# A graph layer whose gathers count on semaphores set up by hand

## The chip, the cores and the metric

The kernel runs on one core of a Trainium2 chip. The time is that of one execution on the device in microseconds; the kernel before took 4658.97 us (median of 3 runs, 4657.78 to 4659.96). Five engines of the core appear below: TensorE (PE in the profile), VectorE (DVE), ScalarE (ACT), GpSimd (POOL) and SyncE (SP). Each works through its own instructions in the order in which they stand, and they wait for each other on semaphores.

## The reference

A message-passing layer with 12,500 nodes and 400,000 edges, which come sorted by their target node. In short:

```python
h = concat(s @ lin1_ws * a / 8, (v @ lin1_wv) * a / sqrt(32))      # 160 numbers per node
hid = silu(edge_scalars @ fc_w1 / 8)                               # 64 per edge
w1, w2, w3, w4, w5 = split(hid @ fc_w2 / 8)                        # 64+64+32+32+32 per edge
es, ev = h_s[src], h_v[src]                                        # the gather
m_s1 = w1 * es * e0;  m_s2 = w4 * dot(ev, e1) / 3
m_v1 = (w2 * es) x e1;  m_v2 = w3 * ev * e0;  m_v3 = w5 * cross(ev, e1) / 2
agg = segment_sum([m_s1, m_s2, m_v1, m_v2, m_v3], dst) / 4
o = agg @ lin2 * a;  pre = (self-connection of x) + o
out = layernorm(x + concat(silu(pre_s[:64]), sigmoid(pre_s[64:96]) * pre_v))
```

`e0` and `e1` are the one and the three components of the 4 edge attributes, `a` a number per node.

## The kernel before

The 400,000 edges are cut into 3125 tiles of 128 edges, one edge per partition. Four tiles make a quad, so the main loop, unrolled in Python, has 782 steps, and 24 tiles make a chunk. Indices and edge attributes are loaded for 48 tiles at a time (`AHEAD`). The order of each engine's instructions is the order in which the program is written; the framework adds the semaphore waits. Dependencies of engines on each other go through semaphores, one per engine; a DMA counts on one of eight lanes (DMASW0 to 7 for those that POOL issues, DMAHW0 to 7 for SP's), and a DMA that uses a lane waits for the one that used it before. Where an instruction needs more waits than it can carry itself, queue instructions (`EVENT_SEMAPHORE`, on the engine's queue: DVEq, POOLq) stand ahead of it and hold the rest.

First the node features are multiplied by `lin1` and written as the table `h_tab` to memory. Then, for each quad:

- POOL issues four gathers (line 476), one per tile, each of 128 rows of 160 numbers, from `h_tab` into a quarter of the buffer `hg`. The pool `deep` has six such buffers. A quad's first gather waits for VectorE, which must have read the buffer's former content; its third gather waits, from the seventh quad on, for the weights of the quad three before it (`weighed_by[n - 3]`, the "pace").
- TensorE computes the weights of the four tiles into PSUM, `pw` (line 551, two banks), from `hid`, the hidden layer that it computes every second quad (line 467) and ACT activates (line 469).
- VectorE compares (line 614) each edge's target, relative to its block of 16 nodes, with 0 to 15, which gives the one-hot matrix; it goes into the same bank as the weights. Then it multiplies weights and gathered rows (`pr`): one instruction of 128x512 for the scalars (line 561) and three of 128x384 for the vectors (line 569). Line 623 multiplies one-hot matrix and edge attributes into `sel`. Line 672 adds up results of earlier blocks.
- Two quads later TensorE multiplies `sel` by `pr` (line 630, `pa`), which is the sum over edges. ACT copies it out (line 863, `sa`), TensorE turns it (line 649), ACT copies that (line 652, `tt`), and TensorE applies the second layer (line 664).

The edge attributes come in the order of memory; `by_slot` (line 597) has ACT put them into the order of the steps, `eas`, once per 48 tiles, by six copies of 128x32, three quads before they are needed. SP reloads the indices (line 160), `eat` and the edge scalars.

Of the kernel before, what the change touches and what calls it, by code (L numbers as in the profile page):

```python
# [21 lines left out]
P = 128  # L22
# [9 lines left out]
W = 16  # L32
Q = 4
KB = 4
SIDE = KB * BT
CT = 2 * SIDE
# [25 lines left out]
def gnn_kernel(  # L62
# [21 lines left out]
    nc = tc.nc  # L84
# [21 lines left out]
    rel = consts.tile([P, TT], I16, name="rel")  # L106
# [60 lines left out]
    def index(t):  # L167
        a0, idx, _ = ahead(t)
        return idx[:, t - a0:t - a0 + 1]
# [67 lines left out]
    with tc.tile_pool(name="nodes", bufs=len(starts)) as nodes, tc.tile_pool(  # L237
        name="nodes_ps", bufs=6, space=PSUM
# [33 lines left out]
        for q in range(4):  # L272
            t0, s = divmod(q * QN, P)
            nc.gpsimd.dma_start(at_k[:P - s, q], attr[s:, t0:t0 + NQ])
            if s:
                m = min(NQ, NT - t0 - 1)
# [67 lines left out]
        for c0, cn, xw, xz in loaded:  # L344
# [7 lines left out]
            n = min(cn, P)  # L352
# [56 lines left out]
    for to, part, pieces, w, r0, c0, by in maps:  # L409
        for k, piece in enumerate(pieces):  # L410
# [3 lines left out]
            m = terms.setdefault((to, part, four), len(terms))  # L414
# [54 lines left out]
                nc.scalar.activation(hid[:k, c], ph[:k, c], AF.Silu, scale=1.0 / math.sqrt(64))  # L469
        return hid  # L470

    def gather(pool, idx, behind=None):

        hg = pool.tile([P, Q, D], F32, name="hg")
        for t, i in enumerate(idx):
            got = nc.gpsimd.indirect_dma_start(  # L476
                out=hg[:, t, :], out_offset=None, in_=h_tab,
                in_offset=bass.IndirectOffsetOnAxis(ap=i, axis=0))
            if behind and behind.get(t) is not None:
                tc.add_manual_dep(got.ins, behind[t], mybir.DependencyInfo(  # L480
                    mybir.DependencyClass.Sync, mybir.DependencyReason.DATA), reason="pace")
        return hg

    own = [n for n in range(OWN + EARLY + 6, len(steps) - 4, OWN) if len(steps[n][2]) == Q]
    by_bytes = h_tab.rearrange("n d -> (n d)").bitcast(U8)
# [102 lines left out]
    def by_slot(t):  # L588

        a0, _, eat = ahead(t)  # L590
        if a0 not in sorted_eat:
            n = min(AHEAD, TT - a0)
            eas = loads.tile([P, AHEAD, 4], F32, name="eas")
            m = n // CT
            for u in range(0, SIDE if m else 0, 2):
                o, i = eas[:, 2 * u:2 * u + 1], eat[:, u:u + 1]
                nc.scalar.copy(
                    bass.AP(tensor=o.tensor, offset=o.offset,
                            ap=[o.ap[0], [4 * CT, m], [4, 2], [8, 2], [1, 4]]),
                    bass.AP(tensor=i.tensor, offset=i.offset,  # L600
                            ap=[i.ap[0], [4 * CT, m], [4, 2], [4 * SIDE, 2], [1, 4]]))
            m *= CT
            for k in range(m, n):
                o = slot_of[a0 + k] - a0
                nc.scalar.copy(eas[:, o], eat[:, k])
            sorted_eat[a0] = eas
        return sorted_eat[a0]

    def one_hot(tiles, pw):

        n = len(tiles)
        t0 = slot_of[tiles[0][0]]
        oh = pw[:, :n, NWT:NWT + W]
        nc.vector.tensor_tensor(oh, rel[:, t0:t0 + n, None].to_broadcast([P, n, W]),  # L614
                                iota[:, None, :].to_broadcast([P, n, W]), op=OP.is_equal)
        return oh

    def select_quad(pool, tiles, oh):

# [160 lines left out]
    with tc.tile_pool(  # L780
        name="fin", bufs=1
    ) as fin, tc.tile_pool(
        name="mine", bufs=2
    ) as mine, tc.tile_pool(
        name="late", bufs=2
    ) as late, tc.tile_pool(name="edge", bufs=2) as edge, tc.tile_pool(
        name="deep", bufs=6
    ) as deep, tc.tile_pool(name="banks", bufs=1, space=PSUM) as banks:
        pw_ps = Banks(banks, "pw", Q * 256, 2)
        pa_ps = Banks(banks, "pa", 512, 2)  # L790
# [196 lines left out]
        with in_order:  # L987
            fetch(0)
            hide(0)
            hide(2)  # L990
            waits = []
            weighed_by, summed_by = {}, {}
            checks = farthest(late)
            for n, (c, i, tiles) in enumerate(steps):
                if 2 <= n < 2 + ZP // 2:
                    for k in range(2):
                        clear(2 * (n - 2) + k)
                if 1 <= n < 10:
                    scale(3)
                if n == 13:  # L1000
                    last_own = own_scalars_vectors(fin, *last_nodes)
                if n == 17:
                    connect_last(misc_ps, *last_nodes, *last_own)
                if n in checks:
                    checks[n]()
                if n == 0:
                    fetch(n + 6)
                fetch(n + LEAD)
                fetch_rows(n)
                hg = hq_of.pop(n) if n in own else gather(  # L1010
                    deep, [index(t) for t, _, _ in tiles], {2: weighed_by[n - 3] if n >= 7 else None})
                pw = weights(pw_ps, hids[c, i // 2], [(half, u - i // 2 * 4) for _, half, u in tiles])
                weighed_by[n] = weighed[-1]

                if n + 4 < len(steps) and not steps[n + 4][1] % 2:
                    hids_due.append((n, n + 4))
                if n + 3 < len(steps):
                    by_slot(steps[n + 3][2][0][0])
                rest = spread_out(n, 0)
                if gates_due and (gates_due[0][0] <= n or n + LATE >= len(steps)):  # L1020
                    assert not rest or n + LATE >= len(steps)
                    rest = [rest, gates_due.pop(0)[1]]
                elif rest:
                    rest = [rest]
                step_on = doing.pop(0) if doing and not turning and not rest and not gates_due else None
                ready = []

                def first(n=n):
                    for gate in reversed(rest or []):
                        if gate:  # L1030
                            gate()
                    ready.extend(add_up(n))

                if n + 3 >= len(steps):
                    while ready or adds and adds[0][0] <= n:
                        ready.extend(add_up(n))
                        add(*ready.pop(0))
                oh = one_hot(tiles, pw)
                sel = select_quad(edge, tiles, oh) if n + 2 >= len(steps) else None
                if n in own:  # L1040
                    hg = hg()
                pr = products(edge, pw, hg, len(tiles), [first, lambda n=n: ready.extend(add_up(n))])
                if not sel:
                    sel = select_quad(edge, tiles, oh)
                for a in ready:
                    add(*a)
                if step_on:
                    step_on()
                begin(n)
                some_rows(SLOTS[1])  # L1050
                waits.append((tiles, pr, sel))
                if n + 1 == len(steps):
                    for blocks, tt in due(maps_due, n):
                        output(n, blocks, tt)
                    for js, whole in due(turns_due, n):
                        turn_blocks(n, js, whole)
                while len(waits) > (2 if n + 4 < len(steps) else 1):
                    sum_up(n, *waits.pop(0))
                if n >= 2:
                    summed_by[n - 2] = summed[-1]  # L1060
                some_rows(SLOTS[2])
                spread_out(n, 1)
                some_rows(SLOTS[3])
            assert not scales and not hids_due and not gates_due
            assert not supply and not any(begun.values())
            nc.gpsimd.drain()
            last_steps = finish(fin, misc_ps, *last_job, most=LAST, pool=deep)
            n = len(steps)
            while waits:
                sum_up(n, *waits.pop(0))  # L1070
            while turns_due or maps_due:
                n += 1
                for blocks, tt in due(maps_due, n):
                    output(n, blocks, tt)
                for js, whole in due(turns_due, n):
                    turn_blocks(n, js, whole)
            assert len(adds) <= NO
# [20 lines left out]
        with tc.For_i(0, n_redo, 1):  # L1098
# [108 lines left out]
```

## Time and profile before

| what | value |
|---|---|
| time, median of 3 runs | 4658.97 us |
| time of the profiled execution | 4659.28 us |
| span of the profiled execution | 4657.5 us |
| TensorE busy, mean granted clock | 3852.9 us (83%), 0.870 |
| VectorE busy | 2369.7 us (51%) |
| ACT busy | 840.2 us (18%) |
| POOL busy | 2995.5 us (64%) |
| share of the DMA engines' time, gathers | 21.8% |
| share of the DMA engines' time, SP's transfers | 12.5% |

The span is the time from the first to the last instruction of the profiled execution; 1.8 us of its time lie outside. A row of a group reads: line, engine, operation, what it writes and reads, count, then busy us in total and ns of one, then the idle time of the engine ahead of such instructions and what ended most of it. "issue" means that nothing which the profile shows was waited for, "remote" that what released the wait can't be named. Matmuls' ends are modelled, and consecutive rows of one engine overlap a little. A row of a timeline reads: start, duration, engine, line, operation, and in brackets the idle time ahead of it and its releaser.

### The profile page before, as it was taken

The numbers are of one execution on the slowest core, as the hardware profiler recorded it, in microseconds if no ns is written. First come the engines' busy times: TensorE is split into PE (matmuls) and PEld (weight loads), VectorE is DVE, ScalarE is ACT, GpSimd is POOL, SyncE is SP. The second block draws the span as 40 slices with busy tenths as digits, with TensorE's granted clock in tenths as the row PEclk, the third lists the DMA queues.
The fourth block names the chain that finished last, engine by engine and source line by source line (L and its number), as shares of the span: only waits on it lengthen the run. The fifth ranks groups of instructions, "written<-read, shape, count | busy, mean of one in ns | idle before, by whom it ended". The sixth has DMA issues, their size and how long they took to land.

```text
span 4657.5 us, 53879 instructions
## 1 busy us (share of the span) xinstructions
PE 3852.9 (83%) x17955; PEld 1891.7 (41%) x17955; DVE 2369.7 (51%) x6412; ACT 840.2 (18%) x1872; POOL 2995.5 (64%) x3172
## 2 busy tenths in 40 slices
PE   5788888888888888888888888887888888888886
PEld 4343444444444334344443444343443444444443
DVE  5544554545545455454554555554554554554454
ACT  1211121211111111111111111111111111111112
POOL 6666666666666666666666666666666666666663
PEclk8888898888888898888888888888888898988888
DMA  6333333333333333333333333333333333333331
GB/s 208 93 79 79 95 86 81 94 78 88 95 78 89 87 84 88 90 84 86 90 85 85 89 88 85 89 87 79 93 88 79 93 80 87 95 78 88 86 87 48
DMA packets 237510, 412.26 MB, mean 89 GB/s; under 512 B 78040, under 2 KB 160961, under 8 KB 237093
## 3 DMA queue, kind: packets, MB, share of 16 engines
q0 software_dynamic: 152960, 266.64, 21.8%
q1 hardware_dynamic: 83668, 141.96, 12.5%
q8 instruction: 143, 2.34, 0.2%
q14 instruction: 145, 1.19, 0.1%
q10 hardware_dynamic: 594, 0.13, 0.0%
HBM read 392.49 MB, written 16.00 MB: 88 GB/s over the span
## 4 chain that ended last, share of the span: by engine, by line
PE 63%; issue 12%; another core or an unknown queue 10%; DVE 9%; DMA 2%; POOL 2%; ACT 1%; DVEq 0%; SPq 0%; ACTq 0%; POOLq 0%
PE pa L630 23%; PE pw L551 17%; PE misc L664 8%; PE misc L467 7%; PE misc L649 6%; DVE pr L569 5%; POOL hg L476 2%; PE misc L721 2%; DMA hg<-h_tab,idx 1%; DVE sel L623 1%; PE misc L717 1%; DVE pr L561 1%; DVE pw L614 1%; DMA xz<-in_xv_t_dram 1%
## 5 line engine op out<-in xcount | busy, mean ns | idle before, releaser
L476 POOL DMA_INDIRECT hg<-h_tab,idx x3125 | 2964.8, 949 | 1601.1 <-issue 824.7
L630 PE MATMUL pa<-pr,sel 128*64 128x416 f32 x6250 | 1546.6, 585 | 122.8 <-issue 118.5
L551 PE MATMUL pw<-w,hid 64*128 64x224 f32 x6250 | 1050.7, 408 | 382.9 <-issue 257.7
L614 DVE TENSOR_TENSOR pw<-rel,iota 128x64 f32<-128x64 int16 x782 | 180.1, 230 | 2143.1 <-remote 1114.7
L569 DVE TENSOR_TENSOR pr<-pw,hg 128x384 f32<-128x384 f32 x2346 | 1153.2, 547 | 0.0
L551 PEld LDWEIGHTS pw<-w,hid 64*128 64x128 f32 x6250 | 644.2, 203 | 1078.8 <-issue 742.1
L630 PEld LDWEIGHTS pa<-pr,sel 128*64 128x64 f32 x6250 | 444.4, 149 | 971.3 <-issue 924.5
L561 DVE TENSOR_TENSOR pr<-pw,hg 128x512 f32<-128x512 f32 x782 | 540.2, 691 | 30.3 <-DVE pw L614 1.9
L467 PE MATMUL misc<-es,w 128*128 128x512 f32 (+1 forms) x784 | 491.3, 709 | 30.5 <-DVE rel L429 19.6
L664 PE MATMUL misc<-tt,l 128*96 128x256 f32 (+5 forms) x1496 | 400.3, 411 | 42.8 <-issue 40.6
L469 ACT ACTIVATE hid<-misc 128x512 f32<-128x512 f32 x392 | 234.4, 598 | 977.3 <-remote 277.7
L652 ACT COPY tt<-misc 128x512 f32<-128x512 f32 (+1 forms) x263 | 153.0, 582 | 1426.5 <-remote 826.8
L863 ACT COPY sa<-pa 128x416 f32<-128x416 f32 x521 | 263.9, 507 | 714.2 <-remote 279.9
L649 PE MATMUL misc<-ident,sa 128*128 128x128 f32 (+1 forms) x1558 | 311.3, 290 | 76.6 <-ACT sa L863 42.3
L623 DVE TENSOR_TENSOR sel<-pw,eas 128x256 f32<-128x256 f32 x782 | 323.2, 413 | 0.1
L664 PEld LDWEIGHTS misc<-tt,l 128*96 128x96 f32 (+1 forms) x1496 | 241.9, 176 | 194.9 <-issue 125.9
L649 PEld LDWEIGHTS misc<-ident,sa 128*128 128x128 f32 x1558 | 218.5, 173 | 162.2 <-issue 100.5
L672 DVE TENSOR_TENSOR acc<-acc,os 96x32 f32 x1042 | 194.1, 186 | 53.4 <-remote 16.3
L467 PEld LDWEIGHTS misc<-es,w 128*128 128x128 f32 x784 | 129.3, 205 | 157.3 <-issue 131.7
L649 PE MATMUL misc<-first_last,sa 128*128 128x128 f32 x784 | 188.8, 297 | 4.3 <-issue 4.2
L717 PE MATMUL misc<-ident,acc 96*128 96x96 f32 x196 | 64.0, 332 | 95.7 <-DVE pw L614 68.3
L667 ACT COPY os<-misc 96x512 f32<-96x512 f32 (+2 forms) x68 | 38.4, 564 | 449.9 <-PE misc L664 168.7
(97 smaller groups left out, 852.1 us busy)
## 6 DMA issues: line engine op xcount, KB each, us to landing
es<-in_es_t_dram SPq DMA_DIRECT2D x258, 384.0 KB
hg<-h_tab,idx POOLq DMA_INDIRECT x3125
h_tab<-ht POOLq DMA_DIRECT2D x24, 320.0 KB
xt<-in_x_dram SPq DMA_DIRECT2D x23, 320.0 KB
out_dram<-y SPq DMA_DIRECT2D x23, 320.0 KB
xv<-in_xv_t_dram SPq DMA_DIRECT2D x23, 192.0 KB
eat<-in_ea_dram SPq DMA_DIRECT2D x41, 96.0 KB
xw<-in_xs_t_dram SPq DMA_DIRECT2D x6, 512.0 KB
```

The lines of the kernel that those rows point to most:

```text
L467: nc.tensor.matmul(ph[:k, c], w1[:k, :k], es[:k, t0 * P + c0 * P:t0 * P + c1 * P], start=True, stop=True)
L469: nc.scalar.activation(hid[:k, c], ph[:k, c], AF.Silu, scale=1.0 / math.sqrt(64))
L476: got = nc.gpsimd.indirect_dma_start(out=hg[:, t, :], out_offset=None, in_=h_tab, in_offset=bass.IndirectOffsetOnAxis(ap=i, axis=0))
L551: weighed.append(nc.tensor.matmul(pw[:, t, :NWT], hid[r, c * P:(c + 1) * P], w2[r], start=True, stop=True).ins.name)
L561: nc.vector.tensor_mul(two, pw[:, :n, :2 * S].rearrange("p t (k c) -> p t k c", k=2), hg[:, :n, None, :S].to_broadcast([P, n, 2, S]))
L569: nc.vector.tensor_mul(pr[:, :n, first:first + V3].rearrange("p t (i c) -> p t i c", i=3), pw[:, :n, None, 2 * S + k * V:2 * S + (k + 1) * ...
L614: nc.vector.tensor_tensor(oh, rel[:, t0:t0 + n, None].to_broadcast([P, n, W]), iota[:, None, :].to_broadcast([P, n, W]), op=OP.is_equal)
L623: nc.vector.tensor_mul(sel[:, :n], oh[:, :, None, :].to_broadcast([P, n, 4, W]), by_slot(tiles[0][0])[:, u:u + n, :, None].to_broadcast([P ...
L630: summed.append(nc.tensor.matmul(pa[half * ROWS:(half + 1) * ROWS, :NPR], sel[:, t].rearrange("p k w -> p (k w)"), pr, start=start, stop=s ...
L649: nc.tensor.matmul(to.rearrange("p (k b w) -> p k b w", k=kinds, b=n), of, moving, start=True, stop=True, is_transpose=kinds == 4)
L664: nc.tensor.matmul(po[:, k, :nb], l2[r, terms[to, part, four]], a[:, :nb], start=(n == 0), stop=(n == len(of) - 1))
L863: nc.scalar.copy(sa, pas.pop(j)[:, :NPR])
```

## The change

Three things are edited.

A quad's gathers no longer count on the eight lanes. The program takes six semaphores of its own, `arrived0` to `arrived5`, one for each buffer of `deep`, and each gather adds 16 to its buffer's semaphore when it lands; the gathers are taken out of the framework's own counting (`no_tile_sem_insts`) and out of its dependencies. Instead the comparison of the quad (line 634 in the new numbering) gets a wait written by hand: for 64 times the number of uses of the buffer so far. The products (line 581) no longer wait for the gathers; they follow the comparison on the same engine.

The gathers keep their waits for VectorE and for TensorE, but have none for a lane's former use. With that, other waits on lanes go too: SP's reload of indices waits for VectorE's comparison in place of all eight lanes. The whole program has 25054 instructions where it had 27851.

The six copies of edge attributes per 48 tiles become one, over the same elements.

What stands in a row of VectorE, before. `pw_512` and `pw_511` are the two PSUM banks of the weights, the first row is the comparison, the second the first product.

```order
L614 TENSOR_TENSOR pw_512<-rel,iota 128x4x16 [waits PE_49]
L561 TENSOR_TENSOR pr<-pw_512,hg 128x4x2x64 [waits DMASW4_49,DMASW3_49,DMASW5_49,DMASW2_49,DVE_49]
L569 TENSOR_TENSOR pr<-pw_512,hg 128x4x96 x3
L623 TENSOR_TENSOR sel<-pw_512,eas 128x256
L672 ISA
```

The same place on VectorE now.

```order
L634 TENSOR_TENSOR pw_512<-rel,iota 128x4x16 [waits PE_49,arrived1]
L581 TENSOR_TENSOR pr<-pw_512,hg 128x4x2x64 [waits DVE_49]
L589 TENSOR_TENSOR pr<-pw_512,hg 128x4x96 x3
L643 TENSOR_TENSOR sel<-pw_512,eas 128x256
L692 ISA
```

The wait for the gathers stands one instruction earlier, as one semaphore instead of four lanes; the order of the instructions is the same. In the built program the comparison carries the wait for `arrived` itself, and its wait for TensorE is a queue instruction ahead of it.

POOL before: the four gathers of one quad, and the first of the next.

```order
L476 DMA hg<-h_tab,idx 128x160 [waits DMASW6_49,DVE_49]
L476 DMA hg<-h_tab,idx 128x160 [waits DMASW7_49]
L476 DMA hg<-h_tab,idx 128x160 [waits DMASW0_49,PE_49]
L476 DMA hg<-h_tab,idx 128x160 [waits DMASW1_49]
L476 DMA hg<-h_tab,idx 128x160 [waits DMASW2_49,DVE_49]
```

The same five gathers on POOL now.

```order
L482 DMA hg<-h_tab,idx 128x160 [waits DVE_49]
L482 DMA hg<-h_tab,idx 128x160
L482 DMA hg<-h_tab,idx 128x160 [waits PE_49]
L482 DMA hg<-h_tab,idx 128x160
L482 DMA hg<-h_tab,idx 128x160 [waits DVE_49]
```

A quad's second and fourth gather have no wait left, its first and third one each. In the built programs POOL has 112 queue instructions for waits where it had 1587, and VectorE 860 where it had 1637.

The diff:

```diff
-    def gather(pool, idx, behind=None):
+    DEEP = 6
+    arrived, uses = [], []
+
+    def gather(pool, idx, behind=None, quad=None):
 
         hg = pool.tile([P, Q, D], F32, name="hg")
+        if quad is not None and len(arrived) < DEEP:
+            arrived.append(tc.alloc_semaphore(f"arrived{quad}"))
+            uses.append(0)
         for t, i in enumerate(idx):
             got = nc.gpsimd.indirect_dma_start(
...
-        return hg
+            if quad is not None:
+                got.then_inc(arrived[quad % DEEP], 16)
+                tc.no_tile_sem_insts.add(got.ins.name)
+                tc.add_to_no_dep_group(f"quad{quad}", got.ins)
+        if quad is None:
+            return hg
+        uses[quad % DEEP] += len(idx)
+        landed = 16 * uses[quad % DEEP]
+
+        def there(first):
+            first._wait_ge(arrived[quad % DEEP], landed)
+            tc.declare_fence(first.ins, group=f"quad{quad}")
+            return hg
+
+        return there
...
-            for u in range(0, SIDE if m else 0, 2):
-                o, i = eas[:, 2 * u:2 * u + 1], eat[:, u:u + 1]
+            if m:
+                o, i = eas[:, 0:1], eat[:, 0:1]
                 nc.scalar.copy(
                     bass.AP(tensor=o.tensor, offset=o.offset,
-                            ap=[o.ap[0], [4 * CT, m], [4, 2], [8, 2], [1, 4]]),
+                            ap=[o.ap[0], [4 * CT, m], [16, SIDE // 2], [8, 2], [1, 8]]),
                     bass.AP(tensor=i.tensor, offset=i.offset,
-                            ap=[i.ap[0], [4 * CT, m], [4, 2], [4 * SIDE, 2], [1, 4]]))
+                            ap=[i.ap[0], [4 * CT, m], [8, SIDE // 2], [4 * SIDE, 2], [1, 8]]))
...
-        nc.vector.tensor_tensor(oh, rel[:, t0:t0 + n, None].to_broadcast([P, n, W]),
+        compared = nc.vector.tensor_tensor(oh, rel[:, t0:t0 + n, None].to_broadcast([P, n, W]),
                                 iota[:, None, :].to_broadcast([P, n, W]), op=OP.is_equal)
-        return oh
+        return oh, compared
...
-                    deep, [index(t) for t, _, _ in tiles], {2: weighed_by[n - 3] if n >= 7 else None})
+                    deep, [index(t) for t, _, _ in tiles], {2: weighed_by[n - 3] if n >= 7 else None}, n)
...
-                oh = one_hot(tiles, pw)
+                oh, compared = one_hot(tiles, pw)
+                hg = hg(compared)
```

More of the change, by code (lines that the diff above doesn't have):

```diff
@@ L786, in gnn_kernel @@
     ) as late, tc.tile_pool(name="edge", bufs=2) as edge, tc.tile_pool(
-        name="deep", bufs=6
+        name="deep", bufs=DEEP
     ) as deep, tc.tile_pool(name="banks", bufs=1, space=PSUM) as banks:
@@ L1037, in gnn_kernel @@
                         add(*ready.pop(0))
-                oh = one_hot(tiles, pw)
+                oh, compared = one_hot(tiles, pw)
+                hg = hg(compared)
                 sel = select_quad(edge, tiles, oh) if n + 2 >= len(steps) else None
-                if n in own:
-                    hg = hg()
                 pr = products(edge, pw, hg, len(tiles), [first, lambda n=n: ready.extend(add_up(n))])
```

## The prediction

> **What bounds the kernel now.** I read the page's first part and its costliest groups, then the chain that ended last, and then, because the chain names POOL only once, what POOL and VectorE waited for. First the page: its line of busy times, its chain by engine, and two of its groups (busy us and mean ns, then idle us before them).
>
> ```profile
> PE 3852.9 (83%) x17955; PEld 1891.7 (41%) x17955; DVE 2369.7 (51%) x6412; ACT 840.2 (18%) x1872; POOL 2995.5 (64%) x3172
> PE 63%; issue 12%; another core or an unknown queue 10%; DVE 9%; DMA 2%; POOL 2%; ACT 1%; DVEq 0%; SPq 0%; ACTq 0%; POOLq 0%
> L476 POOL DMA_INDIRECT hg<-h_tab,idx x3125 | 2964.8, 949 | 1601.1 <-issue 824.7
> L614 DVE TENSOR_TENSOR pw<-rel,iota 128x64 f32<-128x64 int16 x782 | 180.1, 230 | 2143.1 <-remote 1114.7
> ```
>
> By the first two lines TensorE is the bound, at 83% and 63% of the chain. I do not take that at face value, because the gathers alone also fill the whole span. The same gathers by their line (ns min/median/max, first and last start) and the first of them in time order:
>
> ```profile
> L476 POOL DMA_INDIRECT hg<-h_tab,idx x3125: 942/949/1125, 51.3 to 4613.1; - x196
> 51.31 1.05 POOL L476 DMA_INDIRECT hg<-h_tab,idx  x1 [3.20 <-DMA scv<-in_sc_wv_dram]
> 52.67 0.97 POOL L476 DMA_INDIRECT hg<-h_tab,idx  x1 [0.31 <-issue]
> ...
> 56.45 0.95 POOL L476 DMA_INDIRECT hg<-h_tab,idx  x1 [0.30 <-issue]
> ```
>
> 48.1 us before the first gather's own idle time, 2964.8 busy, 1601.1 idle and 43.5 us after the last gather make 4657.5 us, which is the span. So the time is the gathers' busy time, the 0.30 us between any two, and their pauses. What POOL waited for ahead of a gather (us, times, longest):
>
> ```profile
> POOL hg L476 <- issue: 824.7, 2686, 3.2
> POOL hg L476 <- remote: 443.6, 187, 3.1
> POOL hg L476 <- PE pw L551: 146.7, 81, 7.2
> POOL hg L476 <- PE misc L467: 56.5, 36, 4.1
> POOL hg L476 <- PE misc L649: 47.5, 26, 3.0
> POOL hg L476 <- PE pa L630: 22.9, 15, 2.8
> POOL hg L476 <- PE misc L664: 20.8, 8, 2.7
> ```
>
> 2686 of 3125 gathers follow the last one after 824.7/2686 = 0.31 us. The pauses are the other rows, all put down to PE or to a releaser the profile cannot name: 738.0 us in 353 pauses, of which 353 x 0.30 = 106 would be there anyway, so 632 us are real. They fall at a quad's third gather, which waits for the weights of the quad three before it. How long are they? A stretch of POOL's timeline, with the rows inside the two bursts left out:
>
> ```profile
> 2044.68 0.95 POOL L476 DMA_INDIRECT hg<-h_tab,idx  x1 [2.61 <-remote]
> 2045.93 0.94 POOL L476 DMA_INDIRECT hg<-h_tab,idx  x1 [0.31 <-issue]
> ...
> 2058.46 0.95 POOL L476 DMA_INDIRECT hg<-h_tab,idx  x1 [0.30 <-issue]
> 2062.06 0.94 POOL L476 DMA_INDIRECT hg<-h_tab,idx  x1 [2.65 <-PE misc L664]
> ...
> 2070.85 0.95 POOL L476 DMA_INDIRECT hg<-h_tab,idx  x1 [0.30 <-issue]
> 2073.74 0.95 POOL L476 DMA_INDIRECT hg<-h_tab,idx  x1 [1.95 <-PE misc L467]
> ```
>
> The first burst is 12 gathers and takes 17.38 us to the next start; the second is 8 and takes 11.68 us. Four more gathers cost 5.70 us, 1.425 each, with 0.28 us over. Within a burst the rows show 1.25 us. So the pause grows by about 0.17 us with every gather issued: it looks as if each gather costs POOL 1.425 us, of which a row shows 0.95 and the next start 1.25, and the debt is paid before the release is seen. As a check, 51.3 + 3125 x 1.425 + 353 x 0.28 + 43.5 = 4647 us, 0.2% under the span. The Trainium skill ("Perfetto Trace Analysis", DMA Instruction — SWDGE (GPSIMD)) says that a software gather's profile row ends when its last descriptor is written and leaves out what follows; the debt of 0.17 us agrees with that.
>
> The release itself comes late. TensorE's and VectorE's rows around the pause before:
>
> ```profile
> 2016.10 1.03 PE L551 MATMUL pw<-w,hid 64*128 64x224 f32 x8
> 2019.90 0.43 PE L551 MATMUL pw<-w,hid 64*128 64x224 f32 x1 [0.18 <-issue]
> ...
> 2026.93 0.53 PE L551 MATMUL pw<-w,hid 64*128 64x224 f32 x1 [0.85 <-issue]
> 2017.06 0.23 DVE L614 TENSOR_TENSOR pw<-rel,iota 128x64 f32<-128x64 int16 x1 [1.44 <-PE pa L630]
> 2027.09 0.23 DVE L614 TENSOR_TENSOR pw<-rel,iota 128x64 f32<-128x64 int16 x1 [7.03 <-remote]
> 2027.36 0.69 DVE L561 TENSOR_TENSOR pr<-pw,hg 128x512 f32<-128x512 f32 x1
> ```
>
> The same eight passes take 1.03 us at 2016.10 and 7.56 us from 2019.90 to 2027.46, while POOL gathers. The comparison started at 2027.09 and the next gather at 2027.33: both engines were let go together. TensorE's share of the chain is therefore partly time in which it trickles beside the gathers.
>
> **The change, part by part.** *POOL's waits.* Each gather's wait for its completion lane goes; a quad's first gather keeps VectorE's (buffer free), its third keeps TensorE's, its second and fourth wait for nothing. 1475 queue instructions go with them (1587 to 112 in the built programs). Their price, then the queue instructions at the products' line on VectorE, and last how long VectorE sat idle before the products for a gather (us, times):
>
> ```profile
> L476 POOLq EVENT_SEMAPHORE  x1560: 17/17/3217, 47.1 to 4610.4; - x195
> L561 DVEq EVENT_SEMAPHORE  x1562: 21/50/50, 73.7 to 4626.1; - x196
>   DMA hg<-h_tab,idx: 0.3, 1
> ```
>
> The upper bound that these rows give is 1475 x 17 ns = 25 us. The lower bound is zero: the second to fifth gather of all have no lane wait already, and 52.67 to 56.45 is three steps of 1.26 us, as any. Between the two I take half, -12 us. A third value is possible if the hidden 0.17 us belongs to the lane's wait rather than to the gather; that is rival B. A loss has no row for it: no instruction is added on POOL.
>
> *VectorE.* The products lose two queue instructions per quad and wait only for the comparison. The comparison gets an inline wait for the landed gathers, and its wait for TensorE moves into a queue instruction of its own ahead of it. The removed pair lay beside work: from the comparison's start to the products' start is 0.27 us, of which 0.23 are the comparison. So removal gains 0.04 us at most, 782 x 0.04 = 31 us on VectorE, and that engine is idle 2143 us before the comparison; I take nothing. What is added stands between TensorE's release and the comparison. At least 0.05 us by the row of 21/50/50; at most 0.27/2 = 0.13, since two of them fit under 0.27. I take 0.10. What VectorE waited for ahead of the comparison:
>
> ```profile
> DVE pw L614 <- remote: 1114.7, 202, 13.8
> DVE pw L614 <- PE pw L551: 491.8, 167, 8.6
> DVE pw L614 <- PE misc L467: 187.3, 43, 8.6
> DVE pw L614 <- PE misc L649: 165.6, 41, 11.5
> DVE pw L614 <- PE pa L630: 104.7, 36, 6.4
> DVE pw L614 <- PE misc L664: 47.6, 8, 7.3
> ```
>
> 497 quads wait for TensorE there, 2111.7 us together, so 497 x 0.10 = 50 us of VectorE's time is added. It is off the path as long as POOL paces, since the release that POOL waits for is TensorE's and not VectorE's; I take 0 and keep +50 for rival C. Behind the comparison on VectorE stand the products, the select and the adds, so all slide with it; TensorE's sum two quads later is who waits. For the landed gathers the comparison asks 0.27 us earlier than the products did, and they were last awaited once, for 0.3 us.
>
> *ACT.* Six copies of 128x32 become one of 192 elements per partition.
>
> ```profile
> L597 ACT COPY eas<-eat x390: 208/218/240, 71.3 to 4535.3; 128x32 f32<-128x32 f32 x195
> L863 ACT COPY sa<-pa 128x416 f32<-128x416 f32 x521 | 263.9, 507 | 714.2 <-remote 279.9
> ```
>
> The size 192 lies between 0.218 and 0.507 us; on the line through both, 0.34 us. Six cost at most 6 x 0.218 = 1.31 us, so 65 x 0.97 = 63 us of ACT at most are saved. ACT is 18% busy, so POOL's path gains nothing. SP's reload of indices waits for VectorE instead of all lanes; a block of 48 tiles lasts 48 x 1.425 = 68 us and the reload is wanted only in the next, so nothing.
>
> Sum: 4659.3 (the profiled run, whose span is 4657.5; the median of the runs is 4659.0) - 12 = 4647 us. Less than 0.2% (9.3 us), roughly what a measurement of this kernel can tell from no change, lies near, so this case is mostly "same or a little faster".
>
> **Rivals.** *A, the forecast:* the gathers' 1.425 us are untouched. For it: pauses go by gathers issued, and the rows show no dearer step with a lane wait than without. Its own range is 4634 (all 25 us) to 4680 (some of VectorE's 50 us show).
>
> *B, the lane's wait is part of the debt.* The debt of 0.17 us would then go for the gathers that lose all waits: half of them, 1563 x 0.17 = 266 us, giving about 4390 (4659 - 266 = 4393); for all of them 3125 x 0.17 = 531, about 4130, the floor at which POOL's rows (1.25 us) bind. Against it: no row shows where the 0.17 us sit, and TensorE would have to follow at 4 x 1.25 = 5 us per quad though it trickles beside denser gathers. By the skill's page named above, an instruction is pushed into a wait queue and the sequencer then decodes the next, so a satisfied wait would be under the previous gather's work and B would give nothing.
>
> *C, the comparison is on the path.* The extra queue instruction comes after each release, VectorE frees the weights' bank later, TensorE starts the next weights later, and POOL's release moves: 4659 + 50 = 4709. For it: VectorE is 9% of the chain, and the comparison and the gather were released together. It decides as soon as TensorE's weights wait for VectorE's select more often than for their own trickling.
>
> *D, the gathers become last awaited at the comparison.* If each were, each quad would lose the 0.27 us that the comparison used to cover: 782 x 0.27 = 211 us, 4870. Against it: 0.3 us, once. The Trainium skill ("DMA: Bandwidth & Descriptors", Rules for kernel authors) advises to issue a DMA early and wait on its semaphore late, which speaks against moving the wait from the products up to the comparison; the row shows the gathers so early that the rule does not bite.
>
> **How the numbers follow.** A 42%, B 30%, C 25%, D 3%. The time is A's, 4647. Within A I give 17 to faster by over 0.2%, 15 to within it and 10 to slower. Faster is 30 + 17 = 47%, same 15%, slower 10 + 25 + 3 = 38%. The range goes from 4380, which leaves out B's deeper half (some 13%), to 4720, which leaves out D and C's worse part (some 8%). A alone would be 4634 to 4680.
>
> **What would show it.** Right: bursts of 8 and 12 gathers still 11.7 and 17.4 us long, 0.30 us between starts, ACT down by 30 to 60 us busy, and the wait of the comparison still put down to TensorE. B right: 12 gathers in 16.5 us or less, and shorter pauses at the same 1.25 us steps. C right: bursts as long as before but with longer gaps from TensorE's release to the comparison, and more pauses. D right: the landed gathers named ahead of the comparison in many rows. The forecast falls above all if 1.425 us is not the gathers' own but set by how often POOL's or VectorE's queue looks at a semaphore.

## The result, and the profile after

The changed kernel took 4640.35 us (median of 6 runs, 4637.55 to 4647.01) against 4659.47 us (6 runs, 4657.78 to 4660.45). The ratio is 0.9961, 95% interval 0.9949 to 0.9973: 19 us or 0.39% faster. The profiled run has a span of 4635.8 us, 21.7 us less than before.

The page of the changed kernel, its line of busy times and the groups that answer to those shown of before (busy us and mean ns, idle us before them and its main releaser):

```profile
PE 3797.7 (82%) x17955; PEld 1881.7 (41%) x17955; DVE 2369.2 (51%) x6412; ACT 812.0 (18%) x1547; POOL 2995.9 (65%) x3172
L482 POOL DMA_INDIRECT hg<-h_tab,idx x3125 | 2965.1, 949 | 1576.3 <-issue 752.3
L634 DVE TENSOR_TENSOR pw<-rel,iota 128x64 f32<-128x64 int16 x782 | 180.4, 231 | 2083.6 <-remote 1292.3
```

The gathers are as long as before (949 ns), and their idle time fell from 1601.1 to 1576.3 us, by 24.8. That is the whole gain and a little more: from the first gather's start to the last's the kernel is 24.7 us shorter, the first starts 0.9 us later, and what follows the last takes 2.0 us more. What POOL waited for ahead of a gather in the changed kernel (us, times, longest):

```profile
POOL hg L482 <- issue: 752.3, 2464, 0.9
POOL hg L482 <- remote: 488.3, 201, 3.0
POOL hg L482 <- DVE pr L589: 95.9, 292, 7.1
POOL hg L482 <- PE pw L571: 89.8, 55, 3.6
POOL hg L482 <- PE pa L650: 40.4, 31, 2.6
POOL hg L482 <- PE misc L669: 40.4, 23, 2.8
POOL hg L482 <- PE misc L467: 35.4, 24, 2.6
POOL hg L482 <- PE misc L684: 22.6, 9, 2.6
```

The rows of TensorE and of "remote" come to 716.9 us in 343 cases, where they were 738.0 us in 353: 21 us less. VectorE's row (8.2 us in 5 cases before) is large now, but at 95.9/292 = 0.33 us it is the usual step between two gathers, given a name. So the gain lies in the pauses. Two bursts of POOL's timeline, the rows inside them left out:

```profile
2003.40 0.94 POOL L482 DMA_INDIRECT hg<-h_tab,idx  x1 [2.04 <-PE pw L571]
...
2017.19 0.95 POOL L482 DMA_INDIRECT hg<-h_tab,idx  x1 [0.30 <-issue]
2020.72 0.95 POOL L482 DMA_INDIRECT hg<-h_tab,idx  x1 [2.59 <-remote]
...
2034.50 0.94 POOL L482 DMA_INDIRECT hg<-h_tab,idx  x1 [0.30 <-issue]
2038.11 0.94 POOL L482 DMA_INDIRECT hg<-h_tab,idx  x1 [2.67 <-remote]
```

Twelve gathers take 17.32 and 17.39 us, as before. What differs is how often POOL stops. Counted from all starts of gathers in the two traces (a pause is a step over 1.5 us; a burst runs from the first start after a pause to the first after the next):

| | before | after |
|---|---|---|
| step between gathers without a pause | 1.2546 us | 1.2548 us |
| pauses | 328 | 294 |
| bursts of 12 gathers, median length | 152, 17.40 us | 201, 17.36 us |
| bursts of 8 | 130, 11.67 us | 78, 11.68 us |
| bursts of 4 | 28, 6.50 us | 11, 6.54 us |

More bursts of 12 take the place of bursts of 8 and 4. Fewer pauses as such are not the gain: by the mean lengths, which add up to the time as medians do not, a gather takes 1.448 us in bursts of 8 and 1.451 in bursts of 12 before, 1.450 and 1.448 after. Dear are the short bursts: one of 4 takes 6.73 us in the mean before and 6.59 after, 1.65 to 1.68 us per gather. Above 1.45 us per gather, the bursts of fewer than 8 (38 before, 13 after) cost 31 us before and 11 after, and those of 12 are 0.04 us shorter now, which is 7 us. So some 20 of the 24.8 us are short bursts that no longer occur. The gain is even over the run: of eight stretches of 384 gathers each, counted from the 49th gather on, those before took 558.6 to 561.5 us and those after 556.7 to 557.6 us.

Does a gather leave work behind that the pause has to wait for? The DMA packets in the trace before say no: the last packet of a gather ends 2.15 us (median) after the start of its row, for the first gather of a burst as for the twelfth (medians by place from 2.15 to 2.16 us). After a burst of 12 the next gather starts 1.45 us later than that, after a burst of 8 0.73 us. Nor do TensorE's passes simply slow down while POOL gathers. In the 152 bursts of 12 before, TensorE starts 4.2 to 6.0 matmuls per us in the third to tenth us and 0.9 to 1.7 in the fourteenth to seventeenth, which are the last gather and the pause. The pauses grow with the number of gathers, but where that time is spent no row shows.

Last, the lines that the change touched, from the views of the changed kernel by line (ns min/median/max, first and last start):

```profile
L617 ACT COPY eas<-eat x65: 342/343/372, 71.6 to 4513.5; 128x192 f32<-128x192 f32 x65
L482 POOLq EVENT_SEMAPHORE  x85: 17/17/3374, 47.9 to 4579.4; - x85
L634 DVEq EVENT_SEMAPHORE  x782: 21/21/5369, 67.3 to 4605.7; - x196
```

One copy of 0.343 us stands for six of 0.218, POOL's queue has 85 instructions at the gathers for 1560, and each of 782 comparisons has one queue instruction ahead of it.

### The profile page after: what moved, and what is told of

The parts are those of the page before. It is cut to its first block, busy times and chain, and to the rows that moved or that the text cites. A ratio compares the mean times of both kernels' runs of the same rounds, so it can differ in the third digit from the quotient of the medians.

```text
span 4635.8 us, 51082 instructions
## 1 busy us (share of the span) xinstructions
PE 3797.7 (82%) x17955; PEld 1881.7 (41%) x17955; DVE 2369.2 (51%) x6412; ACT 812.0 (18%) x1547; POOL 2995.9 (65%) x3172
## 3 DMA queue, kind: packets, MB, share of 16 engines
q14 instruction: 126, 1.03, 0.1%
## 4 chain that ended last, share of the span: by engine, by line
PE 61%; another core or an unknown queue 15%; issue 10%; DVE 10%; ACT 1%; DMA 1%; DVEq 0%; SPq 0%; ACTq 0%
PE pa L650 22%; PE pw L571 15%; PE misc L684 8%; PE misc L467 7%; PE misc L669 6%; DVE pr L589 6%; PE misc L741 1%; DVE sel L643 1%; DVE pw L634 1%; PE misc L737 1%; DVE pr L581 1%; DMA xz<-in_xv_t_dram 1%; DVE acc L692 1%; ACT sa L883 0%
## 5 line engine op out<-in xcount | busy, mean ns | idle before, releaser
L482 POOL DMA_INDIRECT hg<-h_tab,idx x3125 | 2965.1, 949 | 1576.3 <-issue 752.3
L571 PE MATMUL pw<-w,hid 64*128 64x224 f32 x6250 | 1002.1, 403 | 366.5 <-issue 236.0
L571 PEld LDWEIGHTS pw<-w,hid 64*128 64x128 f32 x6250 | 623.0, 200 | 1016.9 <-issue 680.2
L669 PE MATMUL misc<-ident,sa 128*128 128x128 f32 (+1 forms) x1558 | 328.2, 303 | 127.3 <-ACT sa L883 77.6
L669 PEld LDWEIGHTS misc<-ident,sa 128*128 128x128 f32 x1558 | 230.8, 183 | 226.0 <-issue 119.9
L669 PE MATMUL misc<-first_last,sa 128*128 128x128 f32 x784 | 199.9, 311 | 15.3 <-issue 15.3
L669 PEld LDWEIGHTS misc<-first_last,sa 128*128 128x128 f32 x784 | 121.5, 164 | 15.7 <-issue 15.7
```

Source lines behind the costliest of these rows:

```text
L482: got = nc.gpsimd.indirect_dma_start(out=hg[:, t, :], out_offset=None, in_=h_tab, in_offset=bass.IndirectOffsetOnAxis(ap=i, axis=0))
L571: weighed.append(nc.tensor.matmul(pw[:, t, :NWT], hid[r, c * P:(c + 1) * P], w2[r], start=True, stop=True).ins.name)
L669: nc.tensor.matmul(to.rearrange("p (k b w) -> p k b w", k=kinds, b=n), of, moving, start=True, stop=True, is_transpose=kinds == 4)
```

## The experiments

Ratios are to the kernel before, on the same chip. This matters more than I knew: chips differ. On the chip of the result and on those that the record numbers 11 and 8, the kernel before took 4659, 4710 and 4712 us. On number 5, which the runs from lanes' waits to the first run in stages met, it took 4001 to 4004 us.

### The parts of the change

Two kernels hold one part each. The kernel before with the single copy:

```diff
-            for u in range(0, SIDE if m else 0, 2):
+            if m:
...
-                            ap=[o.ap[0], [4 * CT, m], [4, 2], [8, 2], [1, 4]]),
+                            ap=[o.ap[0], [4 * CT, m], [16, SIDE // 2], [8, 2], [1, 8]]),
```

> The kernel before with only the edge attributes' single copy. If the gain of 19 us is POOL's (1475 queue instructions of 17 ns gone, up to 25 us), this has none of it: 4659, within 4 us. If it is ACT's (28 us less of busy time, so that TensorE gets its inputs sooner and releases POOL sooner), all of it is here: about 4640.

4708.06 us against 4710.38: ratio 0.9996, 0.9987 to 1.0005. The copy is worth nothing that can be measured, though ACT is busy for 807 us here and for 840 in the kernel before.

The changed kernel with the six copies put back:

> The changed kernel with the six copies put back. POOL's queue as the cause: 4640, within 4 us. ACT's copies as the cause: 4659. Half each: 4650.

4694.34 us: ratio 0.9966, 0.9952 to 0.9979. The whole gain is with the semaphores.

Which engine? The changed kernel with the landed gathers awaited by an instruction behind the comparison:

```diff
-        def there(first):
-            first._wait_ge(arrived[quad % DEEP], landed)
-            tc.declare_fence(first.ins, group=f"quad{quad}")
+        def there(_):
+            came = nc.vector.wait_ge(arrived[quad % DEEP], landed)
+            tc.declare_fence(came.ins, group=f"quad{quad}")
             return hg
```

> The changed kernel, with the wait for the landed gathers as an instruction of its own behind VectorE's comparison, where the lanes' waits stood. If my reading is right that VectorE's extra wait ahead of the comparison is off the path, the time stays at 4640 within 5 us. If the 50 us of VectorE's wait were on the path and covered a larger gain, it falls to 4600 or so.

4696.67 us: ratio 0.9968, 0.9956 to 0.998. In this kernel TensorE's wait is carried by the comparison itself again, and the products have two queue instructions ahead of them per quad, as many as before the change. The gain stays. So neither VectorE's number of queue instructions nor the place of its wait makes the gain, and what is left is POOL's waits and SP's few.

The edit also did something on POOL that I had not meant. The gathers' queue instructions in this kernel:

```profile
L482 POOLq EVENT_SEMAPHORE  x795: 17/17/3619, 47.5 to 4647.7; - x199
```

They are 795, where the changed kernel has 85 and the one before 1560: a quad's first gather has a second wait for VectorE, in a queue instruction. Half of what the change took from POOL's queue is thus back, 710 x 17 ns = 12 us by the row's price, or 0.0026 of the ratio, and the ratio is 0.9968 beside 0.9966. So the gain does not go by the number of POOL's queue instructions at this price. The number of pauses does not tell it either: the profiled runs of the single copy alone, of this kernel and of the one with six copies have 357, 346 and 328 pauses and spans of 4697.8, 4697.5 and 4695.0 us.

Put POOL's waits back, then. Each gather waits for what landed in its buffer before, which is long satisfied:

```diff
+                if uses[quad % DEEP]:
+                    got._wait_ge(arrived[quad % DEEP], 16 * uses[quad % DEEP])
                 got.then_inc(arrived[quad % DEEP], 16)
```

> The changed kernel, in which each gather waits again for the buffer's former gathers to have landed, which they have long done: on POOL this is what the lanes' waits were, one satisfied wait for each of 3101 gathers, half of them as a queue instruction. POOL's queue as the cause of the gain: back to 4659 or more. If a satisfied wait is free on POOL: 4640, bursts of 12 gathers at 17.4 us as in both kernels.

4787.32 us: ratio 1.0166, 1.0153 to 1.018, far slower than either kernel. The gathers by line and group, first of this kernel:

```profile
L482 POOLq EVENT_SEMAPHORE  x1560: 17/17/11967, 47.4 to 4732.6; - x195
L482 POOL DMA_INDIRECT hg<-h_tab,idx x3125 | 2956.3, 946 | 1731.2 <-issue 571.5
```

and of the one with six copies on the same chip:

```profile
L482 POOL DMA_INDIRECT hg<-h_tab,idx x3125 | 2965.8, 949 | 1634.5 <-issue 755.6
```

The idle time is 97 us larger, with the same number of queue instructions as in the kernel before (1560). In the built program the reason can be seen: where an instruction can carry one wait, the wait written by hand stayed on the gather and TensorE's went into the queue instruction; before the change the queue instruction held the lane's wait and the gather itself TensorE's. Counted as above, bursts of 12 have a median of 17.93 us against 17.55 in the kernel with six copies, and bursts of 8 12.17 against 11.77: 0.4 us for each pause, and 5.76 against 5.78 us for four gathers more. The satisfied wait costs the step between gathers nothing (1.251 us with it, 1.254 without); the late wait, held one instruction ahead, costs each pause 0.4 us. Kind L in the last run below has satisfied waits on all its gathers too, but the other way round, and shows no such cost (1.463 to 1.469 us per gather where the changed kind has 1.458 to 1.466). This run was not the test I meant. The next put the waits where the lanes' had stood:

```diff
+            former = quad is not None and 16 * uses[quad % DEEP]
+            if former and not t % 2:
+                nc.gpsimd.wait_ge(arrived[quad % DEEP], former)
...
+                if former and t % 2:
+                    got._wait_ge(arrived[quad % DEEP], former)
                 got.then_inc(arrived[quad % DEEP], 16)
```

> The changed kernel with the waits for the buffer's former gathers put back exactly as the lanes' waits stood on POOL: as queue instructions ahead of the first and third gather of a quad, which themselves still carry VectorE's and TensorE's waits, and carried by the second and fourth. In the run with such waits before, the queue instruction held TensorE's wait and each pause grew by about 0.4 us. If satisfied waits on POOL are the change's gain of 0.35%, it is gone: ratio 1.000 to the kernel before. If they are free: 0.996 to 0.997, and no pause is 0.4 us longer.

4001.68 us against 4001.22: ratio 1.0001, 0.9992 to 1.001. This chip has no pauses, so the question stayed open. Again, and it was number 5 again:

> The changed kernel with the lanes' kind of waits back on POOL, once more, since the chip of the first time ran the kernel before in 4001 us without a pause of POOL, where the waits ahead of pauses can show nothing. On a chip with pauses (the kernel before at 4650 to 4710 us): if satisfied waits on POOL are the change's gain, ratio 1.000 to the kernel before; if they are free and the gain is VectorE's, 0.996 to 0.997. On a chip without pauses again 1.000, which tells nothing.

1.0004, 0.9995 to 1.0014. It tells only that on such a chip satisfied waits on POOL cost nothing.

### The wait ahead of the comparison

```diff
-                oh, compared = one_hot(tiles, pw)
-                hg = hg(compared)
+                hg = hg()
+                oh, compared = one_hot(tiles, pw)
```

with `there` as in the run with the wait behind the comparison, so that the queue instruction holds the gathers and the comparison carries TensorE's wait:

> The changed kernel with the landed gathers awaited by a queue instruction ahead of the comparison, and TensorE's wait carried by the comparison itself, as before the change. If the queue instruction that stands between TensorE's release and the comparison in the changed kernel is on the path, this is faster by up to 50 us, ratio 0.985 to 0.990 to the kernel before. If it is off the path, as I forecast: 0.996 to 0.997.

4001.25 us: ratio 1.0, 0.9991 to 1.0009, on a chip without pauses. Its kind came again in stages, below.

### The pace, and a chip without pauses

The changed kernel without POOL's wait for TensorE:

```diff
-                    deep, [index(t) for t, _, _ in tiles], {2: weighed_by[n - 3] if n >= 7 else None}, n)
+                    deep, [index(t) for t, _, _ in tiles], None, n)
```

> The changed kernel without the wait of a quad's third gather for TensorE's weights; POOL then waits only for free buffers. If 1.425 us per gather is the gathers' own, the time can't go under 51 + 3125 x 1.425 + 46 = 4550 us, and bursts, now ended by VectorE's waits, still come to 1.42 us per gather. If the debt of 0.17 us per gather belongs to TensorE's waits, the gathers go at 1.25 us: 4000 to 4400.

4002.03 us: ratio 1.0002, 0.9993 to 1.0011. Once more:

> The changed kernel without POOL's wait for TensorE's weights, once more. On a chip with pauses: if 1.425 us per gather is the gathers' own there, POOL is stopped by VectorE's buffers instead and the time stays above 4550 us, ratio above 0.975; if the debt comes with TensorE's waits on POOL, the gathers go at 1.25 us and the time falls to 4000 to 4200, ratio below 0.90. On a chip without pauses 1.000, as before.

1.0003, 0.9994 to 1.0012. And gathers of half the bytes, which leave out half of each row and so a part of the result:

```diff
-                out=hg[:, t, :], out_offset=None, in_=h_tab,
+                out=hg[:, t, :D // 2], out_offset=None,
+                in_=h_tab.rearrange("n (k d) -> (n k) d", k=2),
...
-                hg[:, :n, S:].rearrange("p t (i c) -> p t i c", i=3))
+                hg[:, :n, None, D // 2 - V:D // 2].to_broadcast([P, n, 3, V]))
```

> The changed kernel with gathers of 80 numbers per edge in place of 160 (half of each row is left out, and the vector products read 32 of them three times over; all counts of instructions stay). If 1.425 us per gather is time that the bytes take on the DMA engines, the pace falls towards the 1.25 us of the rows: about 4100 to 4300. If it is POOL's work per row, which is unchanged at 128 rows per gather: as the changed kernel, within 0.5%.

3998.55 us: ratio 0.9994, 0.9984 to 1.0003. None of the three moves anything here. What such a chip looks like, in the kernel without pace: the page's chain and groups,

```profile
POOL 43%; issue 17%; DMA 13%; DVE 13%; PE 12%; DVEq 0%; ACT 0%; POOLq 0%; ACTq 0%
L482 POOL DMA_INDIRECT hg<-h_tab,idx x3125 | 2959.2, 947 | 955.1 <-issue 888.2
```

VectorE's waits ahead of the comparison,

```profile
DVE pw L634 <- DMA hg<-h_tab,idx: 1181.2, 476, 6.1
DVE pw L634 <- PE pw L571: 301.6, 114, 5.3
```

and TensorE's passes for the weights in its timeline:

```profile
2000.53 1.03 PE L571 MATMUL pw<-w,hid 64*128 64x224 f32 x8
2004.09 1.03 PE L571 MATMUL pw<-w,hid 64*128 64x224 f32 x8
```

The gathers have the same length (947 ns) and the same step: 955.1/3125 = 0.31 us idle between any two. But POOL never pauses. The chain names POOL first, the comparison waits for the gathers 476 times where on the other chips it waits for TensorE, and TensorE does its eight passes in 1.03 us beside running gathers. The 3124 steps of 1.25 us from the first gather's start to the last's are 3910 us; with 53.5 us ahead of the first and 40.4 us from the last one's start to the end that is the span of 4004. Another difference is TensorE's granted clock: 0.91 in all profiles from this chip, 0.855 to 0.874 in those from the others. Whether that is a cause of the pauses or follows from them no run here tells; the clocks differ by 4 to 7%, the times by 16 to 18%. How much TensorE is held up is seen in the idle time ahead of its weights, put down to "issue" (us, times, matmuls and weight loads together), first in the changed kernel on the chip of the result,

```profile
  issue: 916.2, 1227
```

then in the kernel without pace on this chip:

```profile
  issue: 239.8, 308
```

### Six kinds of quads in one run

To have all kinds on one chip I put them into one kernel, in stages of 28 to 52 quads, with the edits shown above (B is the gather on the framework's lanes):

```diff
+    STAGES = [('B', 52), ('A', 52), ('L', 52), ('G', 44), ('N', 32), ('H', 28)]
+    cycle = [k for k, m in STAGES for _ in range(m)]
```

> The changed kernel with its 782 quads in stages of 28 to 52, three rounds of six kinds, so that one chip shows them side by side: B gathers on the framework's lanes and waits as before the change; A as changed; L as changed with the lanes' kind of waits back on POOL; G with the landed gathers awaited ahead of the comparison, which carries TensorE's wait itself; N without POOL's wait for TensorE; H with half of each row gathered (and so a part of the result left out). On a chip with pauses of POOL, by us per gather: B 1.455, A 1.450. L at B if satisfied waits on POOL are the gain, at A if not. G at A if the extra queue instruction on VectorE is off the path, 1.435 if its 50 us show. N 1.42 or more if the pace is the gathers' own, 1.25 if the debt is TensorE's waits. H 1.25 to 1.35 if bytes make the pace, 1.45 if POOL's work per row does. On a chip without pauses all six at 1.25, which says that none of the six costs POOL anything by itself.

3998.74 us, where the kernel before takes 4004.05: a chip without pauses. All three stages of B, A, L, G and N lie between 1.250 and 1.251 us per gather, those of H at 1.250. Half the bytes do not move POOL's step on this chip.

The last run reversed the order and had S for H:

```diff
+            if how == "S" and t == 3:
+                continue
```

> Stages again, in another order: N, G, L, A, B as in the run before, and S, in which a quad's fourth gather is left out (the products read the first tile's rows for all four, so a part of the result is left out). On a chip without pauses: N, G, L, A and B at 1.25 us per gather, and S tells whether POOL's issue is the bound: 3.76 us per quad if it is still, 4.2 to 4.4 if TensorE (3361 us busy of 4004, 4.3 per quad) is next behind it. On a chip with pauses, us per gather: B 1.455, A 1.450, L at B if satisfied waits on POOL are the gain and at A if not, G at A or 1.435, N at 1.42 or more if the pace is the gathers' own and 1.25 if the debt is TensorE's waits, and S 4.3 us per quad.

4647.77 us, the kernel before 4712.13 on the same chip: one with pauses. Busy time of POOL's gathers by stage (L, A, B, S, N and G in this order; length of the stretch, then busy us and number of gathers, TensorE's clock, and the DMA engines' share and GB/s):

```profile
548.00:828.90 280.90, 181.59 (x192) 0.84 0.36 87
853.30:1133.80 280.50, 181.74 (x192) 0.88 0.37 87
1156.30:1438.00 281.70, 181.58 (x192) 0.86 0.35 84
1461.00:1569.50 108.50, 68.17 (x72) 0.95 0.39 93
1595.50:1776.70 181.20, 106.00 (x112) 0.85 0.33 79
1800.40:2036.20 235.80, 151.32 (x160) 0.86 0.35 84
```

Length by number gives the us per gather; of each kind there are three stages, and the first four quads of each are left out:

| kind | us per gather |
|---|---|
| B, as before | 1.467, 1.463, 1.463 |
| A, as changed | 1.461, 1.466, 1.458 |
| L, lanes' kind of waits on POOL | 1.463, 1.469, 1.465 |
| G, gathers awaited first | 1.459, 1.474, 1.473 |
| N, no wait for TensorE | 1.669, 1.617, 1.592 |
| S, three gathers a quad | 1.507, 1.517, 1.488 |

B and A differ by 0.002 in the mean, L and A by 0.004, and stages of one kind among these by up to 0.008 (of G by 0.015), so the run does not tell whether L is B or A. G is no faster than A; the 1.435 of an extra wait on the path is excluded. S takes 4.52 us per quad (108.5/24 steps of three) where A takes 5.84: a gather less saves 1.3 us, though TensorE's work per quad is the same. By bursts: three quads with nine gathers take 13.3 us (mean of 8 bursts), three quads with twelve 17.5 us. So on this chip too the time goes by gathers and not by quads, and with three gathers beside it TensorE does a quad in 4.5 us. Whether a gather takes that time itself or holds up TensorE, for which POOL then waits, S does not separate.

N was to go to 1.25 or stay at 1.42 and more. It rose to 1.6. What POOL waited for in the second of its stages,

```profile
POOL hg L498 <- DVE pr L611: 43.0, 9, 6.4
```

and POOL's timeline there, the inner rows left out:

```profile
1595.60 0.94 POOL L498 DMA_INDIRECT hg<-h_tab,idx  x1 [6.35 <-DVE pr L611]
...
1609.34 0.95 POOL L498 DMA_INDIRECT hg<-h_tab,idx  x1 [0.30 <-issue]
1615.72 0.97 POOL L498 DMA_INDIRECT hg<-h_tab,idx  x1 [5.43 <-DVE acc L715]
1618.52 0.94 POOL L498 DMA_INDIRECT hg<-h_tab,idx  x1 [1.83 <-issue]
...
1641.02 0.95 POOL L498 DMA_INDIRECT hg<-h_tab,idx  x1 [0.30 <-issue]
1648.32 0.94 POOL L498 DMA_INDIRECT hg<-h_tab,idx  x1 [6.36 <-DVE pr L611]
```

Twelve gathers take 20.12 us and nineteen 29.80: 9.68 for seven, 1.38 each, with 3.5 us over. So the debt is there without POOL's own wait for TensorE: 1.38 against the 1.25 of the steps. It may still come by way of TensorE, since VectorE, for which POOL now waits, itself waits for it. What grew is the fixed part of a pause, from 0.28 to 3.5 us. With the pace POOL goes on as soon as TensorE's release is seen; without it, as I read the rows, POOL fills the buffers and then waits until VectorE, let go by such a release, has compared and multiplied (0.23 + 0.69 + 1.48 us by the trace before the change). The wait that looks like the brake is worth some 10% on such a chip by these stages (no whole run without it met one), and nothing on the other.

## Why the prediction was right or wrong

**The bound.** Right in what it says of the change: bursts of 8 and 12 kept their 11.7 and 17.4 us, the step its 1.25 us, without POOL's wait for TensorE the debt remains (N), and a gather less per quad saves 1.3 us (S). The split into 1.425 us per gather and 0.28 per pause came from two bursts. By the means of the whole trace it is 1.45 and nothing, and a burst of 4, which the split puts at 5.98 us, takes 6.50 by the median. Not borne out is that each gather owes 0.17 us of its own. The Trainium skill ("Perfetto Trace Analysis", DMA Instruction — SWDGE (GPSIMD)) has a gather's row end at its last descriptor and leave out the movement of the data. The trace agrees, with rows of 0.95 us and last packets 2.15 us after the row's start. But what follows the row is equally long at every place in a burst, so it is no debt that grows, against what the prediction took from that page. And the growth of the pauses is not a property of the kernel: on chip 5 there is none, and no reading of the one trace could have told.

**POOL's term,** "-12 us", half of the upper bound of 25 us. Mis-sized: the gathers' idle time fell by 24.8 us. That this is near the upper bound of 25 us is luck, since it was not saved as 17 ns here and there: the step is 1.2546 and 1.2548 us, and with 795 queue instructions on POOL the gain was the same as with 85. It came for the most part as fewer short bursts. That the gathers' waits on POOL are the cause is reached by leaving out the rest (copy 0.9996; VectorE's place and number 0.9968, like the change itself) and is not shown directly: the direct runs fell on a chip without pauses, L lies inside the scatter, and SP's waits changed with them, which no run tried alone. Which of these waits it is, and why there are fewer short bursts, is open.

**VectorE's term,** zero with +50 us kept for rival C. Right: the wait behind the comparison gives the same time as ahead of it, and G is not faster than A. The comparison's wait is TensorE's, and one queue instruction more is lost in it.

**ACT's term,** zero. Right; the copy took 0.343 us where the line through two rows gave 0.34, and ACT's busy time fell by 28 us, just under the 30 to 60 I gave.

**Not foreseen:** 0.9 us later at the first gather and 2.0 us more behind the last.

**Rival B** has fallen: the step between gathers and the 5.76 us for four gathers more are the same with a satisfied wait on each gather as without. Times near its floor of 4130 us do occur, but on another chip and with the lanes' waits in place. **Rival D's** condition, gathers last awaited, holds on that chip 476 times (in the kernel without pace), and still the place of the wait is worth nothing there. The likely reason is that POOL's issue sets the end there and the 0.27 us are VectorE's.

## What to carry to other kernels

When an engine's starts have a steady step and its pauses grow with the number of starts before them, fit length against number over bursts of all sizes, by means: the slope says what the time goes by. It does not say where the time is spent; for that, look whether the DMA packets fall behind the rows. When an edit is taken back to find a cause, count the queue instructions of every engine in what was built: here an edit on VectorE put 710 of them back on POOL. Before taking away a wait that the profile blames, ask what stops the engine next: here the blamed wait ended pauses 3 us earlier than the one behind it. And where an instruction has two waits, let it carry the late one itself and have the queue instruction ahead hold the satisfied one; the other way cost 0.4 us at each of some 300 pauses.

## What the runs showed of the hardware

- The same program takes 4001 to 4004 us on one chip and 4659 to 4712 us on the others. Rows of the gathers (946 to 949 ns) and their step (1.25 us) are the same; on the slower ones TensorE's eight passes of 1.03 us can take 7.5 us, its releases come late, POOL pauses, and the time comes to 1.45 to 1.47 us per gather, at a granted clock of 0.855 to 0.874 where number 5 has 0.91. What makes a chip one or the other stays open.
- A gather's last packet ends 2.15 us after the start of its row (median, before the change), at the first place of a burst as at the twelfth.
- Gathers of 128 rows take POOL 0.95 us and start every 1.25 us with rows of 640 bytes and of 320 bytes alike (chip without pauses; not tried on the other kind).
- A queue instruction that holds a late wait ahead of a gather that carries a satisfied one adds 0.4 us to the pause on POOL, and the other way round none showed; on VectorE, ahead of the comparison, no such cost showed in the time.
